# Norms at a batch's end in other places, layer-1 statistics in output frames, and attention sources sent through DRAM

## The chip, the core and the metric

The program runs on one core of one Trainium2 chip. The core has TensorE (matmuls, PE in the profile; its weight loads are PEld), VectorE (DVE), ScalarE (ACT), GpSimd (POOL) and SyncE (SP), which issues most transfers. The metric is the device time of one execution in microseconds (us). The kernel before takes 3635.57 us, the median of three runs (3635.41 to 3636.2). Its profiled execution has a span of 3630.0 us, and TensorE's granted clock was 1.000 of full speed throughout.

## The reference, cut to what matters

Two graph layers on x (8 batches, 2048 nodes, 256 features) with one adjacency matrix (2048 x 2048):

```python
h = relu(layernorm(x))
# layer 0: 4 heads of 64, softmax over each chunk of 256 keys
q, k, v = h @ Wq.T + bq, h @ Wk.T + bk, h @ Wv.T + bv
scores = clip(q k / 8, -10, 10); scores = where(adj == 0, -10, scores)
ctx = sum over 8 chunks of softmax(scores of the chunk) @ v
x = x + layernorm(ctx @ Wo.T + bo + h) * gamma + beta
# layer 1: one head, additive scores
h = relu(layernorm(x)) @ W
e = leaky_relu(e_src[:, None] + e_dst[None, :], 0.01), -1e9 where adj == 0
x = x + relu(softmax(e) @ h)
```

Here e_src and e_dst are h times the two halves of a vector a. In layer 1 a weight exp(leaky_relu(s + d)) is built, up to a factor that cancels, as the larger of two products: a source row times a number of the target, against another number of the target. So the kernel needs, for each block of 512 nodes, the source values exp(0.99 s) as one row of 512 that is repeated on all 128 partitions.

## The kernel before

**Blocks and batches.** A batch's 2048 nodes are four blocks of 512 (`NB`), each four tiles of 128 (`TB`). The blocks are named zero, low, mid and last. For each batch the kernel runs the attention of layer 0, then a stretch that is called the batch's end here, then the products of layer 1. While a batch is in layer 0 or in its end, the projections of the next one (`ahead`) are made.

**Attention.** It has 32 steps (4 blocks x 8 chunks). A frame f, made of `begin(f)` and `end(f)`, holds logits of step f-1, clips (VectorE, L449), exps (ScalarE, L458), sums of pairs of exps (GpSimd, L464), values matmuls of steps f-2 and f-3 (L425), the reciprocal of the sum (L469, L470), the scaling (VectorE, L479) and, from a block's second chunk on, a transfer that adds the scaled product `prod` to `ctxT` (GpSimd's queue, L484). There is one buffer for `prod`.

**Places.** Other work is put into the frames by a hand-written list: `at(n, piece)` puts a piece at place n, where place 2f is the first half of frame f and 2f+1 its second half. A block takes 16 places (`PER`), attention 64 (`STEPS2`). The kind of a piece says where in the half frame it runs: `first` ahead of everything, `pe` beside the matmuls, `mid` between two clips, and without a kind late in the frame's second half (in front of two exps for an even place, behind the logits for an odd one).

**Beside the frames.** `Between` is one block's work after its attention: `residual` (ScalarE relus of the normed input, L291), `bias`, `output_tiled` (projection by Wo, L633), `take_tiles`, `stats`, `power`, `shift`, `scaled` (layer norm), `gamma`, `beta`, `add`. Then come the statistics for layer 1: `stats1` (VectorE, two instructions for each tile, L268 and L269), `power1` (ScalarE), `shift1` (GpSimd within frames) and `norm1` (ScalarE relus). `beside` lists these for blocks zero, low and mid at places counted from the next block's start. The output projection lies at places 8 and 9, so in each later block there is one output frame, in which TensorE has about 3.8 us more to do. The last block's pieces stand in the program's main loop, from place 64 on, and behind the frames.

**Layer 1.** `values` and `keep` make the rows `g` and the two numbers of each node, `sd[:, 0]` (source) and `sd[:, 1]` (target). These have nodes on partitions. `sources(nb)` turns the source column of a block into a row on all partitions: four transposes on TensorE of a column that is repeated 128 times (L815) into one bank of PSUM, and an exp on ScalarE (L819) into a tile `src` of the tag `hn`, which has five buffers. `weights` (VectorE, L825 and L831) makes four tiles of weights from `src`, and `products` (TensorE, L848) multiplies them with `g`. Each block has four such pieces, 16 for a batch, with weights made two pieces ahead. `finish` scales the sums, adds the mean for nodes without neighbours and adds to x on GpSimd (L865). Blocks 0 and 1 have their `sources` at the batch's end in seven batches (`ahead` exists), blocks 2 and 3 in the loop, at the second piece of the block before. In the last batch that of block 1 stands before the first products.

**Queues.** Each engine runs its instructions in the order of the program. SP's queue issues loads of x and of the mask `bound`, stores of the output, and empty instructions (`fence`, L381) that order matmuls which write one bank.

Of the kernel before, what the change touches and what calls it, by code (L numbers as in the profile page):

```python
# [8 lines left out]
F32 = mybir.dt.float32  # L9
# [8 lines left out]
P = 128  # L18
# [10 lines left out]
def gnn_two_layers(  # L29
# [38 lines left out]
    def ps_s():  # L68
        return ps.tile([P, 2, 512], F32, tag="s", name="ps_s")
# [10 lines left out]
    def ps_m():  # L80
        if turn_about[0]:
            turn_about[1] += 1
            if turn_about[1] % 2:
                return ps_n()
        return ps_t()
# [28 lines left out]
    kept = ctx.enter_context(tc.tile_pool(name="kept", bufs=1, space=bass.MemoryType.DRAM))  # L114
    bound_d = [kept.tile([P, NT, NB], I8, name=f"bound_d{nb}") for nb in range(NNB)]
    bounds, bounds1 = {}, {}

    def bound_tile():
        return xpool.tile([P, NT, NB], I8, tag="bound", name="bound", bufs=2)
# [472 lines left out]
    class Between:  # L592
# [151 lines left out]
        def beside(self):  # L744

            todo = {
                -3: [self.load],
                3: [lambda: self.residual(0)],
                4: [lambda: self.residual(1)],
                5: [lambda: self.bias(0)],  # L750
                6: [lambda: self.bias(1)],
                8: [pe(lambda: self.output_tiled(0)), lambda: self.stats([0]), lambda: self.beta(0)],
                9: [
                    pe1(lambda: self.output_tiled(1)), mid_clips(lambda: self.take_tiles(0)),
                    mid_clips(lambda: self.take_tiles(1)), lambda: self.stats([1]),
                ],
                10: [lambda: self.stats([2]), lambda: self.beta(1)],
                11: [lambda: self.stats([3])],
                12: [self.power],
                13: [self.shift],  # L760
                14: [lambda: self.scaled(range(TB))],
                15: [lambda: self.gamma(0)],
                16: [lambda: self.gamma(1)],
                18: [lambda: self.add(0)],
                20: [lambda: self.add(1)],
            }

            def at(n, *pieces):
                todo.setdefault(n, []).extend(pieces)

            if self.nb == NNB - 2:
                return todo
            for t, n in enumerate((20, 22, 26, 28)):
                at(n, lambda t=t: self.stats1([t]))
            at(29, self.power1)
            at(30, self.shift1)
            if self.nb == 1:
                at(31, lambda: self.norm1(0))
                at(32, lambda: self.norm1(1))
            return todo  # L780


    class Layer1:
# [21 lines left out]
        def targets(self, t0=0, t1=NT):  # L805
            d = self.sd[:, 1, t0:t1]
            nc.scalar.activation(self.cd[:, 0, t0:t1], d, AF.Exp)
            nc.scalar.activation(self.cd[:, 1, t0:t1], d, AF.Exp, scale=SLOPE, bias=negshift)

        def sources(self, nb):  # L810

            pt = ps_m() if nb < 2 or nb % 2 else ps_s()[:, 0, :]
            for i in range(TB):
                t = TB * nb + i
                nc.tensor.transpose(  # L815
                    pt[:, i * P:(i + 1) * P], self.sd[:, 0, t:t + 1].to_broadcast([P, P]), ident
                )
            self.src[nb] = work.tile([P, NB], F32, tag="hn", name="src", bufs=5)
            nc.scalar.activation(self.src[nb], pt, AF.Exp, scale=1.0 - SLOPE, bias=negshift)  # L819
# [33 lines left out]
        def finish(self, nb, accs, store=False):  # L853
            x4 = self.blocks[nb].x4
            for t in range(TB):
                acc = accs[t]
                rz = small.tile([P, 1], F32, tag="rz1", name="rz1")
                nc.vector.tensor_scalar(rz, acc[:, F:F + 1], 1e-37, None, op0=ALU.max)  # L858
                nc.vector.reciprocal(rz, rz)
                r = work.tile([P, F], F32, tag="r", name="r")  # L860
                nc.scalar.activation(r, acc[:, 0:F], AF.Relu, scale=rz)
                nc.vector.scalar_tensor_tensor(
                    r, self.average, lone[:, nb * TB + t:nb * TB + t + 1], r, op0=ALU.mult, op1=ALU.add
                )
                nc.gpsimd.tensor_tensor(x4[:, t, :], x4[:, t, :], r, op=ALU.add)  # L865
                if store:
                    at = (nb * TB + t) * P
                    nc.sync.dma_start(out[self.b, at:at + P, :], x4[:, t, :])
# [122 lines left out]
    for b in range(B):  # L991
# [40 lines left out]
        at(3 * PER + 4, lambda: fetch(bounds1, 0))  # L1032
        at(STEPS2 + 2, lambda: fetch(bounds1, 1))
        at(STEPS2 - 6, last.load)
        at(STEPS2 - 1, lambda: last.residual(0))

        late = 0 if ahead else 3
        at(STEPS2 + late, lambda: last.residual(1))
        at(STEPS2 + 1, lambda: last.bias(0))
        at(STEPS2 + 2 + late, lambda: last.bias(1))  # L1040
        at(STEPS2 + 3, lambda: last.beta(0))
        at(STEPS2 + 4, lambda: last.beta(1))
        at(STEPS2 + 2, pe(lambda: low.turn1(0)), pe(lambda: low.turn1(1)))
        at(STEPS2 + 3, first(lambda: low.keep1(0)), first(lambda: low.keep1(1)))
        if ahead:
# [32 lines left out]
        if ahead:  # L1078
            for t in range(TB):
                mid.stats1([t])  # L1080
                low.values(t)
                low.keep(t)
            mid.power1()
            mid.shift1()
            ahead.load(2)
            ahead.turn(1, 0)
            ahead.turn(1, 1)
            mid.norm1(0)
            mid.norm1(1)
            ahead.norm(2, 0)  # L1090
            ahead.values(0)
            last.output(0)
            last.output(1)
            last.take(0)
            last.take(1)
            ahead.norm(2, 1)
            ahead.load(3)
            mid.ends(0)
            last.stats(range(TB))
            ahead.qk(1, 0)  # L1100
            last.power()
            last.shift()
            last.scaled(range(TB))
            ahead.qk(1, 1)
            for t2 in range(2):
                last.gamma(t2)
                last.add(t2)
            for t in range(TB):
                last.stats1([t])
                mid.values(t)  # L1110
                mid.keep(t)
            last.power1()
            last.shift1()
            ahead.turn(2, 0)
            ahead.turn(2, 1)
            last.norm1(0)
            last.norm1(1)
            ahead.values(1)
            zero.norm1(0)
            zero.norm1(1)  # L1120
            ahead.norm(3, 0)
            ahead.qk(2, 0)
            zero.ends(0)
            ahead.norm(3, 1)
            ahead.qk(2, 1)
            zero.ends(1)
            ahead.turn(3, 0)
            ahead.turn(3, 1)
            ahead.values(2)
            last.ends(0)  # L1130
            ahead.qk(3, 0)
            last.ends(1)
            one.total()
            one.targets()
            one.sources(0)
            one.sources(1)
            ahead.qk(3, 1)
            weights(0)
            one.mean()
            weights(1)  # L1140
            ahead.values(3)
        else:
            for t in range(TB):
                zero.values(t)
                zero.keep(t)
                mid.stats1([t])
            one.targets(0, TB)
            one.sources(0)
            mid.power1()
            mid.shift1()  # L1150
            low.ends(1)
            weights(0)
            mid.norm1(0)
            mid.norm1(1)
            one.targets(TB, 2 * TB)
            last.output(0)
            last.output(1)
            weights(1)
            last.take(0)
            last.take(1)  # L1160
            mid.ends(0)
            mid.ends(1)
            last.stats(range(TB))
            last.power()
            last.shift()
            last.scaled(range(TB))
            one.targets(2 * TB, 3 * TB)
            one.sources(1)
            accs[0] = one.accumulators(0)
            early(0)  # L1170
            for t2 in range(2):
                last.gamma(t2)
                last.add(t2)
            last.stats1(range(TB))
            last.power1()
            last.shift1()
            weights(2)
            last.norm1(0)
            last.norm1(1)
            early(1)  # L1180
            last.ends(0)
            last.ends(1)
            early(2)
            one.total()
            one.targets(3 * TB, NT)
            weights(3)
            one.mean()
            weights(4)

        far = projs[b + 2] = Projection(b + 2) if b + 2 < B else None  # L1190
        for i, (nb, j4) in enumerate(pieces1):
# [3 lines left out]
                weights(i + 2)  # L1195
            if nb not in accs:
                accs[nb] = one.accumulators(nb)
            if j4 == 1 and nb + 1 < NNB and nb + 1 not in one.src:
                one.sources(nb + 1)
            one.products(accs[nb], ws.pop(i), j4)  # L1200
            if j4 == 0 and nb > 0:
                one.finish(nb - 1, accs[nb - 1])
# [53 lines left out]
```

The softmax here doesn't subtract the row's maximum and nothing guards it: scores larger than these inputs give would overflow.

## Time and profile before

| from the profile of the kernel before | us |
|---|---|
| span | 3630.0 |
| TensorE busy | 3594.1 |
| VectorE busy | 2577.4 |
| ScalarE busy | 1961.8 |
| GpSimd busy | 1791.5 |
| attention of the second batch, 983 to 1229 us: TensorE busy | 246.00 of 246.00 |
| products of the second batch, 872.46 to 963.5 us: TensorE busy | 91.04 of 91.04 |
| last batch's end, 3475 to 3530 us: TensorE busy | 48.42 of 55.00 |
| first 90 us: TensorE busy | 70.88 of 90.00 |

The rows for stretches come from a table by stage of the trace. A row of a group of instructions reads: line, engine, operation, output and inputs by their names, shapes, count, then the busy time in us and the mean length of one in ns, and then idle time of the engine just before them with what ended it. A listed length of a matmul spans its way through the pipeline, and matmuls overlap: what one takes of TensorE's stream is the distance from its start to the next one's start. A row of the timeline reads: start in us, length in us, engine, line, operation, tiles, count, and in brackets the idle time before it.

### The profile page before, as it was taken

The page shows a single profiled execution, that of the slowest core. Times are in us where ns is not written, and L with a number is a line of the kernel's source. Part 1 is how long each engine was busy: PE and PEld are TensorE (multiplying, and loading weights), DVE is VectorE, ACT ScalarE, POOL GpSimd, SP SyncE. Part 2 cuts the span into 40 slices and gives each one's busy share as a digit, 9 for nine tenths or more (in the row PEclk, how much of TensorE's full clock was granted, in tenths as well). Part 3 has the DMA queues.
Part 4 walks back from the last instruction along what each step waited for, and adds up shares of the span by engine and source line. Part 5 has one row for each costly group of instructions (what it writes and reads, how often), then busy time and mean ns, then how long its engine had stood idle before and what let it go on. Part 6 is the DMA issues. An engine that isn't in the chain of part 4 may idle for free.

```text
span 3630.0 us, 104929 instructions
## 1 busy us (share of the span) xinstructions
PE 3594.1 (99%) x46640; PEld 2205.1 (61%) x46640; DVE 2577.4 (71%) x3963; ACT 1961.8 (54%) x2975; POOL 1791.5 (49%) x1142
## 2 busy tenths in 40 slices
PE   7999999999999999999999999999999999999999
PEld 4444785547745577555874458645586555864568
DVE  5887577866778666786667866678576785757866
ACT  5677416774167732677236762377713767146650
POOL 0678016870178702786037850378403784047731
PEclk9999999999999999999999999999999999999999
DMA  7444113340134411343113431134312442124321
GB/s 226 116 103 101 41 53 84 83 108 28 64 84 87 98 37 57 84 101 83 47 48 83 101 77 47 53 84 95 79 51 59 89 90 59 47 54 89 76 55 35
DMA packets 133302, 277.27 MB, mean 76 GB/s; under 512 B 26608, under 2 KB 91888, under 8 KB 124656
## 3 DMA queue, kind: packets, MB, share of 16 engines
q0 software_dynamic: 32256, 117.45, 17.7%
q1 hardware_dynamic: 83952, 151.01, 12.2%
q8 instruction: 365, 5.98, 0.7%
q10 hardware_dynamic: 16640, 2.10, 0.4%
q14 instruction: 89, 0.73, 0.1%
HBM read 132.12 MB, written 20.97 MB: 42 GB/s over the span
## 4 chain that ended last, share of the span: by engine, by line
PE 97%; DMA 1%; ACT 1%; DVE 1%; issue 0%; POOL 0%; ACTq 0%; POOLq 0%; SPq 0%; DVEq 0%
PE ps_s L409 24%; PE ps_n L425 24%; PE ps_s L848 12%; PE ps_t L437 6%; PE ps_n L848 6%; PE ps_t L848 6%; PE ps_t L633 2%; PE ps_t L353 2%; PE ps_n L353 2%; PE ps_s L353 2%; PE ps_t L721 2%; PE ps_n L721 2%; PE ps_t L367 1%; PE ps_n L367 1%; PE ps_t L300 1%; PE ps_n L300 1%
## 5 line engine op out<-in xcount | busy, mean ns | idle before, releaser
L464 POOL TENSOR_TENSOR both<-e 128x1024 f32<-128x1024 f32 x512 | 1219.8, 2411 | 646.9 <-PE ps_t L437 340.1
L449 DVE SCALAR_TENSOR_TENSOR e<-ps_s,bound 128x1024 f32<-128x1024 f32 x1024 | 1223.7, 1220 | 404.6 <-PE ps_s L409 401.5
L409 PE MATMUL ps_s<-q,k 64*32 64x512 f32 x16384 | 1434.1, 590 | 2.1 <-DVE e L449 2.1
L458 ACT ACTIVATE e<-e 128x1024 f32<-128x1024 f32 x1024 | 1050.5, 1051 | 545.4 <-DVE e L449 529.6
L425 PE MATMUL ps_n<-e,v 64*32 64x512 f32 x16384 | 1220.5, 590 | 4.8 <-ACT e L458 2.3
L425 PEld LDWEIGHTS ps_n<-e,v 64*32 64x32 f32 x16384 | 451.9, 107 | 482.1 <-issue 391.9
L409 PEld LDWEIGHTS ps_s<-q,k 64*32 64x32 f32 x16384 | 451.9, 106 | 468.2 <-issue 325.4
L865 POOL TENSOR_TENSOR x<-x,r 128x256 f32<-128x256 f32 x128 | 98.7, 771 | 1135.9 <-DVE rz L858 1004.8
L437 PE MATMUL ps_t<-both,ones 64*32 64x512 f32 x4096 | 539.0, 591 | 0.6
L848 PE MATMUL ps_s<-g,w 128*128 128x257 f32 x2048 | 448.6, 380 | 0.0
L848 PEld LDWEIGHTS ps_s<-g,w 128*128 128x128 f32 x2048 | 387.7, 190 | 55.5
L479 DVE TENSOR_TENSOR prod<-ps_n,rz 128x512 f32<-128x512 f32 x448 | 288.5, 686 | 169.1 <-PE ps_n L425 85.1
L831 DVE SCALAR_TENSOR_TENSOR w<-bound,w 128x1024 f32<-128x1024 int8 x256 | 313.7, 1225 | 8.7
L848 PE MATMUL ps_n<-g,w 128*128 128x257 f32 x1024 | 292.4, 382 | 0.0
L848 PE MATMUL ps_t<-g,w 128*128 128x257 f32 x1024 | 289.7, 380 | 0.0
L825 DVE TENSOR_SCALAR w<-src,cd 128x512 f32<-128x512 f32 x512 | 265.3, 561 | 9.8 <-ACT src L819 9.4
L469 ACT ACTIVATE rz<-ps_t 128x512 f32<-128x512 f32 x256 | 153.0, 598 | 166.5 <-PE ps_t L437 128.4
L484 POOL DMA_DIRECT2D ctxT<-prod x224 | 194.7, 869 | 52.5 <-DVE prod L479 50.9
L848 PEld LDWEIGHTS ps_n<-g,w 128*128 128x128 f32 x1024 | 192.2, 190 | 43.9 <-issue 17.6
L848 PEld LDWEIGHTS ps_t<-g,w 128*128 128x128 f32 x1024 | 193.8, 189 | 28.1
L437 PEld LDWEIGHTS ps_t<-both,ones 64*32 64x32 f32 x4096 | 115.2, 106 | 92.7 <-SPq L381 47.0
L470 ACT ACTIVATE rz<-rz 128x512 f32<-128x512 f32 x256 | 161.8, 632 | 8.1
(130 smaller groups left out, 2882.3 us busy)
## 6 DMA issues: line engine op xcount, KB each, us to landing
ctxT<-prod POOLq DMA_DIRECT2D x224, 512.0 KB, 4.8
bound<-bound_d SPq DMA_DIRECT2D x62, 1024.0 KB, 5.1
xp<-in_x_dram SPq DMA_DIRECT2D x60, 512.0 KB, 4.6
rows<-in_adj_dram SPq DMA_DIRECT2D x32, 512.0 KB, 5.2
x<-in_x_dram SPq DMA_DIRECT2D x32, 512.0 KB, 4.7
out_dram<-x SPq DMA_DIRECT2D x31, 512.0 KB, 2.9
bound_d<-bound_part ACTq DMA_DIRECT2D x16, 128.0 KB, 4.5
bound_d<-bound SPq DMA_DIRECT2D x2, 1024.0 KB, 6.2
```

The lines of the kernel that those rows point to most:

```text
L353: nc.tensor.matmul(pp, w[:, di, do * P:(do + 1) * P], self.hT[nb][:, di, :], start=di == 0, stop=di == FC - 1,)
L409: nc.tensor.matmul(self.s[n, o][c * Q:(c + 1) * Q, kt, :], self.k[p][rows, at:at + Q], self.q[p][rows, nb * NB:(nb + 1) * NB], start=True, ...
L425: made.append(nc.tensor.matmul(self.num[n, c][h * Q:(h + 1) * Q, :], self.v[rows, j * KT + kt, at:at + Q], self.e[n, p][rows, i * KT + kt, :],
L437: nc.tensor.matmul(self.total[n][h * Q:(h + 1) * Q, :], ones[rows, :], self.both[n, h // 2][rows, h % 2, :], start=half == 1, stop=half == 0,)
L449: nc.vector.scalar_tensor_tensor(self.e[n, p][:, i * KT:(i + 1) * KT, :], self.s.pop((n, o)), -CLIP * SC, bounds[nb][:, j * KT:(j + 1) * K ...
L458: nc.scalar.activation(e, e, AF.Exp, scale=1.0 / SC)
L464: nc.gpsimd.tensor_tensor(self.both[n, p], e[:, 0], e[:, 1], op=ALU.add)
L479: nc.vector.tensor_tensor(dst[:, c, :], self.num.pop((n, c)), self.rz[n], op=ALU.mult)
L484: nc.gpsimd.dma_start(self.ctxT[nb], self.prod.pop(n), accum_op=ALU.add)
L825: nc.vector.tensor_scalar(w[:, i, :], self.src[nb], self.cd[:, 0, j:j + 1], self.cd[:, 1, j:j + 1], op0=ALU.mult, op1=ALU.max,)
L831: nc.vector.scalar_tensor_tensor(two, bounds1[nb][:, j - 1:j + 1, :], 0.0, two, op0=ALU.is_gt, op1=ALU.mult)
L848: nc.tensor.matmul(accs[t][:, 0:F + 1], w[:, i, t * P:(t + 1) * P], g[:, j, :], start=j == 0, stop=j == NT - 1,)
```

## The change

It has four parts.

1. **Sources by transfers.** `sources` stays for block 0 of each batch. For blocks 1, 2 and 3, `send` writes the source column (128 partitions x 4 numbers) to a small tensor in DRAM in the order of the nodes, `receive` loads it as one row of 512 to all partitions, straight into a `src` tile, and `received` takes the exp in place on ScalarE. It is for doing this turn without TensorE and PSUM.
2. **Layer-1 statistics.** `stats1` of blocks zero and low moves from places 20, 22, 26 and 28 to one tile at 22 and three at 25, which is the second half of the next block's output frame, ahead of its clips. `power1` and `shift1` come three places earlier, and so does `norm1` of block low. It is for using frames in which VectorE has less to do than TensorE.
3. **Norms at the batch's end.** The last block's `residual`, `bias` and `beta` come one place later (in the last batch the second `residual` and `bias` stay where they are), so that fewer of ScalarE's norms stand at one place.
4. **The last stores.** In the last batch's last block the addition to x runs on VectorE in place of GpSimd.

```diff
+    source_d = [kept.tile([TB, P], F32, name=f"source_d{nb}") for nb in range(NNB)]
...
-            for t, n in enumerate((20, 22, 26, 28)):
-                at(n, lambda t=t: self.stats1([t]))
-            at(29, self.power1)
-            at(30, self.shift1)
+            at(22, lambda: self.stats1([0]))
+            at(25, first(lambda: self.stats1([1, 2, 3])))
+            at(26, self.power1)
+            at(27, self.shift1)
             if self.nb == 1:
-                at(31, lambda: self.norm1(0))
-                at(32, lambda: self.norm1(1))
+                at(28, lambda: self.norm1(0))
+                at(29, lambda: self.norm1(1))
...
+        def send(self, nb):
+            nc.sync.dma_start(source_d[nb].rearrange("t p -> p t"), self.sd[:, 0, TB * nb:TB * (nb + 1)])
+        def receive(self, nb):
+            self.src[nb] = work.tile([P, NB], F32, tag="hn", name="src", bufs=5)
+            nc.sync.dma_start(
+                self.src[nb], source_d[nb].rearrange("(o t) p -> o (t p)", o=1).to_broadcast([P, NB])
+            )
+        def received(self, nb):
+            src = self.src[nb]
+            nc.scalar.activation(src, src, AF.Exp, scale=1.0 - SLOPE, bias=negshift)
...
-            pt = ps_m() if nb < 2 or nb % 2 else ps_s()[:, 0, :]
+            pt = ps_m()
...
-                nc.gpsimd.tensor_tensor(x4[:, t, :], x4[:, t, :], r, op=ALU.add)
+                adder = nc.vector if store else nc.gpsimd
+                adder.tensor_tensor(x4[:, t, :], x4[:, t, :], r, op=ALU.add)
...
-        at(STEPS2 - 1, lambda: last.residual(0))
-        late = 0 if ahead else 3
-        at(STEPS2 + late, lambda: last.residual(1))
-        at(STEPS2 + 1, lambda: last.bias(0))
-        at(STEPS2 + 2 + late, lambda: last.bias(1))
-        at(STEPS2 + 3, lambda: last.beta(0))
-        at(STEPS2 + 4, lambda: last.beta(1))
+        at(STEPS2, lambda: last.residual(0))
+        late = 0 if ahead else 2
+        at(STEPS2 + 1 + late, lambda: last.residual(1))
+        at(STEPS2 + 2, lambda: last.bias(0))
+        at(STEPS2 + 3 + late, lambda: last.bias(1))
+        at(STEPS2 + 4, lambda: last.beta(0))
+        at(STEPS2 + 5, lambda: last.beta(1))
...
             zero.ends(1)
+            one.send(1)
+            one.send(2)
...
             last.ends(0)
+            one.receive(1)
             ahead.qk(3, 0)
             last.ends(1)
...
             one.sources(0)
-            one.sources(1)
             ahead.qk(3, 1)
             weights(0)
             one.mean()
             weights(1)
+            one.send(3)
+            one.receive(2)
             ahead.values(3)
...
-            one.sources(1)
+            one.send(1)
+            one.receive(1)
             accs[0] = one.accumulators(0)
...
             one.mean()
+            one.received(1)
+            one.send(2)
+            one.send(3)
+            one.receive(2)
...
-            if j4 == 1 and nb + 1 < NNB and nb + 1 not in one.src:
-                one.sources(nb + 1)
+            if j4 == 1 and nb + 1 < NNB:
+                one.received(nb + 1)
+            if j4 == 2 and nb == 1:
+                one.receive(3)
```

## The prediction

> **What bounds the kernel now.** First the page: busy shares, the line of TensorE in the 40 slices, and the chain.
>
> ```profile
> PE 3594.1 (99%) x46640; PEld 2205.1 (61%) x46640; DVE 2577.4 (71%) x3963; ACT 1961.8 (54%) x2975; POOL 1791.5 (49%) x1142
> ...
> PE   7999999999999999999999999999999999999999
> ...
> PE 97%; DMA 1%; ACT 1%; DVE 1%; issue 0%; POOL 0%; ACTq 0%; POOLq 0%; SPq 0%; DVEq 0%
> ```
>
> TensorE is busy or owns the chain nearly everywhere, and the one weak slice is the start, which the change leaves alone. So the questions are: which TensorE instructions leave, and which of its waits change?
>
> Second, TensorE's own groups and the timeline around the instructions that leave (start, length in us):
>
> ```profile
> L815 PE MATMUL ps_n<-ident,sd 128*128 128x128 f32 x64 | 9.6, 272 | 0.0
> L815 PE MATMUL ps_t<-ident,sd 128*128 128x128 f32 x32 | 5.0, 274 | 0.3 <-DVE sd L730 0.3
> L815 PE MATMUL ps_s<-ident,sd 128*128 128x128 f32 x32 | 4.8, 273 | 0.0
> ```
>
> ```profile
> 461.58 0.60 PE L848 MATMUL ps_t<-g,w 128*128 128x257 f32 x2
> 462.01 0.60 PE L815 MATMUL ps_s<-ident,sd 128*128 128x128 f32 x4
> 462.45 0.60 PE L848 MATMUL ps_n<-g,w 128*128 128x257 f32 x2
> ```
>
> A group of four transposes starts at 462.01 and its successor at 462.45: it takes 0.44 us of the stream, though each is listed at 272 to 274 ns. The groups at 418.67, 419.11 and 490.22 have the same distance; finer starts give 0.435 us. Nothing waits before or after them, so they are pure cost.
>
> Third, the waits (waiter, releaser: us in total, times, longest):
>
> ```profile
> DVE prod L479 <- DMA ctxT<-prod: 55.8, 58, 7.2
> ...
> DVE stats L268 <- POOL x L691: 9.0, 7, 1.3
> ```
>
> The first is the only wait that spreads into TensorE within attention: a late accumulate of ctxT holds `prod`, then ps_n, then the next values matmuls. The second is at each batch's end, beside other TensorE work.
>
> Fourth, one output frame on VectorE:
>
> ```profile
> 758.56 1.23 DVE L449 SCALAR_TENSOR_TENSOR e<-ps_s,bound 128x1024 f32<-128x1024 f32 x1 [2.10 <-PE ps_s L409]
> ```
>
> VectorE stands idle for 2.10 us before the second clip of that frame, because TensorE is doing the output projection.
>
> **What the Trainium skill says.** (1) Perfetto Trace Analysis, Identifying the Most-Contended Engine: matmul busy time is a poor measure of distance to roofline, since matmuls are pipelined. The trace agrees (a listed 273 ns against a spacing of 109 ns), so I price by starts. (2) TensorE: Matmul & The Clock Gate, Part 2, Step-by-step: back to back, a matmul costs about one cycle for each column. The spacings agree: 128 columns 109 ns, 257 columns 217 ns. (3) The same page, Part 4: a PE transpose measured about 275 ns, mostly access latency; the listed 273 ns agree, and are not the price here. (4) DMA: Bandwidth & Descriptors, Specifications: transfers under 512 B are read-modify-write. The new send writes 4-byte elements; no run here shows that.
>
> **The change, part by part.**
>
> *Transposes.* 128 run; only block 0 of each batch keeps its four. 8 batches x 3 blocks = 24 groups x 0.435 us = **10.4 us** off TensorE. In the seven batches with a successor, all three groups stand in an unbroken stream (PE idle before L815 is 0.3 us over all). In the last batch they start at 3506.45, 3547.9 and 3575.79, also with products right behind. I count all 24.
>
> *Send and receive in their place.* 48 transfers on SP's queue. What waits on them: the exp in `received` on ScalarE, then the weights on VectorE. Nearest rows: a 1 KB column load lands in 3.9 to 4.3 us, a row broadcast to 128 partitions in 4.4 to 5.6 us. Taking the larger twice, 11.2 us from send to data; the lower end, an out_dram store of 128 KB (1.7) plus 4.2, is 5.9. Block 1's receive can be issued from about 411 us in the first batch (transposes of `last.ends(0)` at 410.88), so its data are there by 422. ScalarE reaches that exp after `mean` (424.04) and is then idle for 16.9 us; VectorE reads the block-1 source first at 442.24. Slack 18 us. Blocks 2 and 3 are asked for more than 10 us ahead (block 3 one block step of 20 us, three pieces of 6.95 us). Even at four times my lower end nothing waits. Taken: 0.
>
> Behind these transfers on SP: the x loads of the batch after next, which run as early as 402 us now and will be issued at about 420. Their reader, a statistic on VectorE, is at 439.10; a load lands in 4.6 us. The fences of attention also pass through SP's queue, but none stands between a send and its receive. 0.
>
> The exp itself: 0.67 to 0.68 us from PSUM before, the same size from SBUF after. 0.
>
> *Layer-1 statistics.* Four pairs (0.42 + 0.18 us, one each 0.53 us) go from places 20, 22, 26, 28 of a block to 22 and 25 (a place is half a frame). The three at place 25 need about 1.7 us and fit into the hole of 2.10 us shown above; behind them wait the clip, and for the clip the logits, so they cost nothing as long as they stay under it. The relieved places had extra statistics and VectorE waits on `prod`. Summing, over all half frames of 3.86 us, what the eight batches have above the best of them, I get about 13 us of scattered stalls, mostly 0.2 to 1 us where a ctxT accumulate landed late. GpSimd's order, which causes most of them, hardly changes. I take 0.5 us off, bounds +4 and -6.
>
> *Norms at the batch's end.* Two relus (1.08 us) of ScalarE leave place 63 for 64, and four of block 1 leave 63 and 64 for 60 and 61. In seven batches TensorE shows no wait there beyond transitions between tiled and full matmuls (0.4 to 0.7 us each), which stay: 0. In the last batch there is less beside work. The bias on GpSimd (3473.20, 1.24 us to the next start) stands before the pair of adds and the last-but-one ctxT transfer (3479.09). Moved behind it, the second add still needs an exp that ends at 3476.02, so the transfer leaves at about 3478.4: 0.7 us earlier, and TensorE waits for exactly this (1.43 us before the transposes at 3485.41). **0.7 us**, bounds 0 and 1.4. The extra relus at 60 and 61 could cost the last batch up to 1 us, because its block 0 norms stand at 58 and 59; I leave that in the range.
>
> *Last add on VectorE.* After the last matmul the chain is max, reciprocal, relu, multiply-add, add, store, and the store of 128 KB lands in 1.7 us. GpSimd's add takes 0.72 us from 3626.58; VectorE's 128x256 adds take 0.42 us (L648) and need no hop. **0.4 us**, bounds 0.2 and 0.6.
>
> Sum: 10.4 + 0.5 + 0.7 + 0.4 = 12.0; 3635.6 - 12.0 = **3623.6 us**.
>
> **The rivals.**
>
> A: the scattered stalls shrink too. For it: VectorE's waits on the transfer are 58, and fewer statistics per place let it catch up. Against: the transfer's landing, not VectorE, ends those waits. Half of 13 us more: about 3617.
>
> B: TensorE is freed, but the time comes back as waits: ScalarE's crowded places 60 and 61 (in one frame of 7.7 us the four exps of 1.05 and the reciprocal's 0.60 and 0.63, 5.4 us, plus four relus and one `power`, 2.9 us) delay exps by about 1 us in each of 8 batches. Against: places 62 and 63 now hold more (scaled, two pairs of relus, a copy) and show no TensorE wait. 3623.6 + 8 = about 3631.5.
>
> C: slower. A send of 512 four-byte writes takes some 30 us instead of 5, or holds SP's queue; then ScalarE waits in `received`, the weights stop, and the products with them: at 2 us per batch 3640, at 4 us 3656. Against: the slack of 18 us, and that column loads with the same four-byte elements land in 4.3 us. Taken at 3642.
>
> **From these to the numbers.** Forecast 0.75, A 0.10, B 0.08, C 0.07. The forecast's own width is its bounds: -6 to +4 from stalls, about 1 from the last batch. The range 3618 to 3629.5 takes in nearly all of it and a part of A. Faster by over 0.2% means under 3628.3: the forecast and A, 0.85. Within 0.2%: B, 0.08. Slower: C, 0.07.
>
> **What would show it.** L815 with 32 transposes; the loop of layer 1 from the first product to the last shorter by 0.87 us in each batch, and the batch's end by 0.44; ScalarE's wait for the source transfer near zero in all but odd cases; PE's idle sum unchanged within 2 us; no TensorE wait on VectorE in output frames. It is wrong if weights wait for the source transfers, if a clip of place 25 holds the logits, or if stalls on ctxT change by more than 5 us.

## The result, and the profile after

| | us |
|---|---|
| before, median of six runs | 3635.49 (3630.91 to 3636.81) |
| after, median of six runs | 3622.85 (3619.28 to 3624.78) |
| after / before | 0.9966, 95% interval 0.9953 to 0.9978 |
| difference | -12.6, forecast -12.0 |
| span of the profiled executions | 3630.0 before, 3622.7 after |

The forecast held. But the single profiled execution gained only 7.3 us, and the way to its sum is not quite the one that was forecast. Line numbers below are those of the kernel whose profile is shown: a line of before stands some lines further down in the changed kernel. The page of the changed kernel, read in the same order as before: busy shares, TensorE in 40 slices, the chain, and from the table of issues (tiles, queue, operation, count, KB each, us to landing) the transfers of the sources.

```profile
PE 3587.4 (99%) x46544; PEld 2202.7 (61%) x46544; DVE 2580.6 (71%) x3967; ACT 1960.9 (54%) x2975; POOL 1788.1 (49%) x1138
...
PE   8999999999999999999999999999999999999999
...
PE 96%; DMA 2%; ACT 1%; DVE 1%; issue 0%; POOL 0%; ACTq 0%; SPq 0%; DVEq 0%; POOLq 0%
...
src<-source_d SPq DMA_DIRECT2D x24, 256.0 KB, 4.8
```

TensorE runs 96 matmuls fewer and still bounds the kernel; DMA's part of the chain went from 1% to 2%. A receive lands in 4.8 us (median; 3.0 to 10.7). From the trace's own table of issues the send, and from the groups of TensorE and ScalarE the transposes and the two kinds of exp:

```profile
source_d<-sd SPq DMA_DIRECT2D x24, 2.0 KB, 8.9
```

```profile
L832 PE MATMUL ps_t<-ident,sd 128*128 128x128 f32 x32 | 5.0, 274 | 0.3 <-DVE sd L732 0.3
...
L825 ACT ACTIVATE src<-src,negshift 128x512 f32<-128x512 f32 x24 | 17.1, 712 | 0.0
...
L836 ACT ACTIVATE src<-ps_t,negshift 128x512 f32<-128x512 f32 x8 | 5.4, 670 | 0.0
```

A send of 2 KB takes 8.9 us (median; 7.9 to 11.1), longer than any other transfer of that table, the largest of which have 1024 KB. Its packets are over 1.2 to 2.4 us after the issue; what is late is the signal that they have landed. Still ScalarE never stood idle ahead of L825 (the last column is 0.0): the slack was enough. So far the plan worked. The waits of the changed kernel (waiter, releaser: us in total, times, longest) show what did not:

```profile
DVE prod L481 <- DMA ctxT<-prod: 38.8, 50, 1.6
...
DVE stats L270 <- POOL x L693: 9.0, 7, 1.3
...
DVE w L842 <- ACT src L825: 3.4, 1, 3.4
...
PE ps_n L723 <- DVE o L658: 3.1, 1, 3.1
PE ps_t L613 <- DMA ctxT<-prod: 3.0, 1, 3.0
```

The last line is new. L613 is the output projection of a last block, and it happened in one batch of eight, the fourth. (`PE ps_n L723 <- DVE o L658: 3.1`, in the last batch, was there before too. `DVE w L842 <- ACT src L825: 3.4` is in the last batch as well and is no wait for a transfer: that source had landed at 3500.6, but its exp stands behind `mean`, whose matmuls start at 3526.47. TensorE did not wait there.)

**By stage.** I measured from the start of a batch's last half frame with logits to the next batch's first; this is the batch's end with its layer 1, and it holds all the 24 removed groups of transposes but the last batch's three.

| stretch | before | after |
|---|---|---|
| up to the first logits | 69.3 | 71.8 |
| attention, eight batches | 2198.9 | 2197.8 |
| batch's end and layer 1, each of six batches | 171.38 | 169.71 |
| the same, fourth batch | 171.38 | 174.51 |
| last batch, to the start of the last matmuls | 156.67 | 155.02 |
| after that | 5.40 | 5.29 |

The first row is not the change's: over the profiled executions of all kernels it lies between 69.3 and 72.3, without order. Six batches gained 1.67 us each. The fourth lost 3.13, that is 4.8 us against its neighbours. Here is its timeline, GpSimd's queue and SP's queue first, then TensorE:

```profile
1703.77 0.87 POOL L486 DMA_DIRECT2D ctxT<-prod  x1 [7.53 <-DVE prod L481]
```

```profile
1707.28 0.37 SPq L815 DMA_DIRECT2D source_d<-sd  x1
```

```profile
1713.46 3.50 PE L613 MATMUL ps_t<-woT,ctxT 128*128 128x256 f32 x8 [3.03 <-DMA ctxT<-prod]
1716.80 1.89 PE L613 MATMUL ps_n<-woT,ctxT 128*128 128x256 f32 x8
```

The last accumulate of ctxT leaves at 1703.77. The DMA records say the rest: its semaphore counts 16 times, as many as the page gives the core DMA engines; 15 counts are in by 1708.31, and the last data packet ends by 1708.6, but the 16th count comes at 1713.33. In between, at 1707.28, SP issued the first send, whose 512 four-byte packets moved from 1708.1 to 1708.8. TensorE waits 3.03 us, and then it is slow: the eight matmuls from 1713.46 take 3.34 us to the next group's start, where the same group takes 1.73 in a batch without the wait. The windows (stretch, us, busy us and count of PE, PEld, DVE, ACT, POOL, then PE clock, DMA share, GB/s) show the clock in the column before the last two. First one of before, in the same stretch of its fourth batch's end, then two of the changed kernel:

```profile
1710.00:1715.00 5.00, 5.00 (x25) 4.36 (x24) 2.02 (x4) 3.53 (x8) 0.00 (x0) 1.00 0.00 0
```

```profile
1710.00:1715.00 5.00, 1.97 (x7) 1.33 (x6) 0.69 (x1) 1.57 (x4) 0.00 (x0) 0.82 0.04 3
1715.00:1720.00 5.00, 5.00 (x24) 4.12 (x23) 1.93 (x5) 1.92 (x5) 0.00 (x0) 0.84 0.00 0
```

So 3.0 us of wait cost 3.0 + 1.6 us. The Trainium skill, TensorE: Matmul & The Clock Gate, Part 1, What's actually happening, says that an idle window of about 3.4 us halves TensorE's clock until a busy window has passed. The trace agrees in kind: 3.03 us of wait were enough here, and the matmuls behind it took 3.34 / 1.73 = 1.9 times as long. The length does not agree: in a later run of the same kernel (e3) 2.4 us were enough (0.82 and 0.84 again), while 2.0 us in e1 left the clock at 1.00.

**Why the fourth batch.** In five of the seven batches the last packet of that ctxT transfer ends 4.2 us after its issue, and the first packet of the send starts at 4.37 to 4.40: they miss each other by 0.2 us. In the fourth batch the last packet ends at 4.8, among the packets of the send. It is late there in 11 of the 13 profiled executions (4.5 to 4.8 us, with and without sends), each time with a packet of an instruction load that starts 1.4 to 2.0 us after the issue; in the two without such a packet (e7 and e8 below) it ends at 4.2. To overlap the send is not enough by itself: in the fifth batch the last packet was later still (5.5) and its count came 0.3 us behind it, as usual. That difference stays open.

**The same on one queue.** The receive of block 2 leaves 0.5 us behind the send of block 3. In all eight batches its data packets are over 2.8 to 4.7 us after its issue, but it counts as landed only at 8.5 to 10.7, 0.2 to 0.8 us behind the send; the other 16 receives land at 3.0 to 6.2. This cost nothing, because that source is not yet needed.

### The profile page after: what moved, and what is told of

Read it like the earlier page. It is cut to its first block, busy times and chain, and to the rows that moved or that the text cites. A ratio compares the mean times of both kernels' runs of the same rounds, so it can differ in the third digit from the quotient of the medians.

```text
span 3622.7 us, 104823 instructions
## 1 busy us (share of the span) xinstructions
PE 3587.4 (99%) x46544; PEld 2202.7 (61%) x46544; DVE 2580.6 (71%) x3967; ACT 1960.9 (54%) x2975; POOL 1788.1 (49%) x1138
## 4 chain that ended last, share of the span: by engine, by line
PE 96%; DMA 2%; ACT 1%; DVE 1%; issue 0%; POOL 0%; ACTq 0%; SPq 0%; DVEq 0%; POOLq 0%
PE ps_s L411 24%; PE ps_n L427 24%; PE ps_s L865 12%; PE ps_t L439 6%; PE ps_n L865 6%; PE ps_t L865 6%; PE ps_t L635 2%; PE ps_t L355 2%; PE ps_n L355 2%; PE ps_s L355 2%; PE ps_t L723 2%; PE ps_n L723 1%; PE ps_t L369 1%; PE ps_n L369 1%; PE ps_t L302 1%; DMA ctxT<-prod 1%
## 5 line engine op out<-in xcount | busy, mean ns | idle before, releaser
L842 DVE TENSOR_SCALAR w<-src,cd 128x512 f32<-128x512 f32 x512 | 265.2, 560 | 10.7 <-ACT src L836 6.9
L275 ACT ACTIVATE krn<-mv,eps 128x4 f32<-128x4 f32 x32 | 9.5, 296 | 292.7 <-DVE mv L271 292.7
L439 PEld LDWEIGHTS ps_t<-both,ones 64*32 64x32 f32 x4096 | 115.2, 106 | 85.8 <-SPq L383 42.4
```

The lines of the kernel that those rows point to most:

```text
L439: nc.tensor.matmul(self.total[n][h * Q:(h + 1) * Q, :], ones[rows, :], self.both[n, h // 2][rows, h % 2, :], start=half == 1, stop=half == 0,)
L842: nc.vector.tensor_scalar(w[:, i, :], self.src[nb], self.cd[:, 0, j:j + 1], self.cd[:, 1, j:j + 1], op0=ALU.mult, op1=ALU.max,)
```

## The experiments

The theory was: the transposes give what was forecast; the send's small packets hold back the count of the ctxT transfer in the fourth batch; and the remaining gain of 0.35 us in a batch comes from the norms, not from the transposes. The main rivals were that the fourth batch's loss is chance, or that it is due to the norms' and statistics' new places. A ratio is to the kernel before on the same chip.

**One part of the change at a time.** The first kernel has part 1 alone, the second parts 2, 3 and 4 without it.

```diff
 e1: as after, but
-            at(22, lambda: self.stats1([0]))
-            at(25, first(lambda: self.stats1([1, 2, 3])))
+            for t, n in enumerate((20, 22, 26, 28)):
+                at(n, lambda t=t: self.stats1([t]))
...
-        at(STEPS2, lambda: last.residual(0))
+        at(STEPS2 - 1, lambda: last.residual(0))
...
 e2: as after, but
-            one.send(1)
-            one.send(2)
...
+            one.sources(1)
```

> The kernel before with the source transfers alone (statistics, norms and last add as before). Theory 1, each group of four transposes costs its distance between starts: 24 x 0.435 = 10.4 us less than before, about 3625 us, TensorE's stretch from the last logits of a batch to the next batch's first shorter by 1.30 us; in some executions one stall of up to 5 us more behind the last ctxT transfer of a batch. Rival, the gain comes from the statistics and norms: within 2 us of before. Rival, the transfers cost what they save: within 2 us of before, with waits for the source tiles on ScalarE or VectorE.

> The other three parts without the transfers; all sources by transposes. Theory 1: 1 to 4 us less than before, of which about 0.35 us per batch are seen between the last logits and the next batch's first, and 0.4 us in the last add. Rival, the statistics and norms carry the result: 10 us or more less. Rival, they cost time: slower than before.

Transfers only: 3627.83, ratio 0.9977 (0.9968 to 0.9986), -8.4 us where 10.4 were expected. In five batches the stretch is 170.05 or 170.06 (170.22 in the seventh), so 171.38 - 170.06 = 1.32 us for three groups of transposes, against a forecast of 3 x 0.435 = 1.30. The fourth batch again stands out, with 172.28: its 16th count took 8.5 us from the issue and TensorE waited 2.0.

The rest only: 3632.49, ratio 0.9989 (0.9982 to 0.9995), -4.0 us; all seven stretches are 171.02 to 171.04, the count of the fourth batch took 5.1 us and nothing waited. So the late count comes with the transfers, not with parts 2 to 4, and the 0.35 us comes with the latter. They add up: 171.38 - 1.32 - 0.35 = 169.71, which is what the whole change has.

In the last batch, from the transposes behind the first 64 products to the last products, every kernel with transposes takes 103.85 or 103.86 us and every one with transfers (except e9 and e10, which change this stretch) 102.97 or 102.98, 0.88 for two groups. As a whole it is no help: up to its last matmuls e1 takes 157.7 and e2 158.4 us, both longer than before's 156.67, and in both the clock from 3500 to 3530 us is 0.89 (1.00 before), behind that batch's wait of 3.1 us.

**The changed kernel again, and the sends in the other order.** `send(1)` can leave early, because the values of block low (`low.keep1`) are ready long before those of block mid. Behind `send(2)` it must wait for those.

```diff
             zero.ends(1)
-            one.send(1)
             one.send(2)
+            one.send(1)
             ahead.turn(3, 0)
```

> The changed kernel itself, for its spread on this chip: two groups, near 3620 and near 3624.5 us, the upper where one wait of TensorE for the last ctxT transfer of a batch (3 us, then 1.6 us at a lower clock) occurred. If there are no two groups, the wait is not what spreads the times.

> The changed kernel with the sends of blocks 2 and 1 swapped in seven batches, so that SP holds the first send until block 2's numbers exist, some 19 us later, when the last ctxT transfer has landed. Theory 2, the four-byte writes of the send hold back the last of the 16 counts of that ctxT transfer: no stall of TensorE before the output projection of the last block, executions near 3620 us, none near 3624.5; median 2 to 4 us under the changed kernel. Rival, the late transfer is chance and has nothing to do with the send: the same spread and median as the changed kernel. Rival, the later send makes the source late: block 1's exp waits, slower.

The changed kernel: 3625.23, ratio 0.9972 (0.9962 to 0.9983); the fourth stretch 173.98, 16th count after 8.9 us, wait 2.4 us. Swapped: 3622.16, ratio 0.9960 (0.9948 to 0.9973); in the profiled execution both sends leave at 1728.96, all seven stretches are within 169.70 and 169.72, the count takes 5.0 us, and L613 has no wait:

```profile
1706.51 0.87 POOL L486 DMA_DIRECT2D ctxT<-prod  x1 [7.55 <-DVE prod L481]
```

```profile
1728.96 0.92 SPq L815 DMA_DIRECT2D source_d<-sd  x2
```

```profile
1713.01 1.89 PE L613 MATMUL ps_t<-woT,ctxT 128*128 128x256 f32 x8
1714.74 1.89 PE L613 MATMUL ps_n<-woT,ctxT 128*128 128x256 f32 x8
```

The trace is clear about the wait. The medians differ by 3.1 us as they should, but these two intervals overlap, so by time alone it isn't shown here. Two expectations failed: the changed kernel's seven runs (3622.0 to 3630.5) do not fall into two groups, and two of the five swapped runs lie above 3624.5. One of these, 3626.22, is the profiled execution that has no late count: its attention took 2205.3 us, 7.5 more than that of the changed kernel's first profile. So the scattered stalls of attention spread the times at least as much as the late count does.

**Which of the other parts gives 0.35 us.**

```diff
 e5: before, with part 2 alone
+            at(25, first(lambda: self.stats1([1, 2, 3])))
...
 e6: before, with part 3 alone
+        at(STEPS2, lambda: last.residual(0))
...
```

> The kernel before with only the layer-1 statistics moved (and power1, shift1 and block low's norm1 three places earlier). Theory 1: TensorE's output frames keep their 5.93 us, since three pairs fit into the hole of 2.10 us; the stretch from a batch's last logits to the next batch's first loses at most 0.35 us of 171.38; scattered stalls of attention stay between 0 and 4.5 us per batch; total 0 to 3 us under before. Rival: the clip behind the three pairs comes late, output frames longer than 5.93 us, slower. Rival: fewer scattered stalls, 5 us or more under before.

> The kernel before with only the residual, bias and beta of the last block moved. Theory 1: the stretch between attention of two batches shorter by 0 to 0.35 us in seven batches, last batch's end shorter by about 0.7 us (the wait of 1.4 us before the second turn of block zero); total 0.5 to 3 us under before. Rival: no change at all, the relus and the bias were hidden in every batch.

Statistics only: 3631.42, ratio 0.9987 (0.9978 to 0.9995). Norms only: 3631.03, ratio 0.9989 (0.9982 to 0.9995). By medians that is 3.8 and 4.1 us less than before, where 0 to 3 and 0.5 to 3 were expected; e6's last batch, expected shorter, took 157.3 us in its profile (156.67 before), at a clock of 0.94 from 3500 to 3530 us. Each alone has stretches of 171.02 or 171.03, and together (e2) 171.02 to 171.04: either one removes the same 0.35 us, 2.4 in seven batches. The rest of these differences is not explained. It can be followed at the end of the second batch. ScalarE's timeline there, first before, then after:

```profile
793.89 1.08 ACT L291 ACTIVATE hn<-x,rn 128x256 f32<-128x256 f32 x2
794.87 1.09 ACT L291 ACTIVATE hn<-x,krn 128x256 f32<-128x256 f32 x2
795.86 1.99 ACT L458 ACTIVATE e<-e 128x1024 f32<-128x1024 f32 x2
```

```profile
793.27 1.08 ACT L293 ACTIVATE hn<-x,krn 128x256 f32<-128x256 f32 x2
794.81 2.19 ACT L460 ACTIVATE e<-e 128x1024 f32<-128x1024 f32 x2 [0.46 <-DVE e L451]
```

and TensorE's values groups beside them:

```profile
789.57 2.00 PE L425 MATMUL ps_n<-e,v 64*32 64x512 f32 x32
...
796.88 0.63 PE L425 MATMUL ps_n<-e,v 64*32 64x512 f32 x4
```

```profile
789.87 2.00 PE L427 MATMUL ps_n<-e,v 64*32 64x512 f32 x32
...
796.76 0.63 PE L427 MATMUL ps_n<-e,v 64*32 64x512 f32 x4
```

Before, four relus stand ahead of the two exps, and the values group at 796.88 starts when the first exp is done (795.86 + 1.05 = 796.91; 1.05 us is the mean of an exp on the page). After, two relus are left, the exp waits for its clip instead and is done at 795.86, nearly a microsecond ahead of the group. From group to group it is 7.31 us before and 6.89 after, and to the transposes that follow (799.47 and 799.42) 9.90 and 9.55: the 0.35 us. Before, both `norm1` of block low (part 2) and `residual` of block last (part 3) brought relus to this spot, which fits that taking either away is enough.

**The send's packets by themselves.** The kernel before, with 24 additional transfers that nobody reads, each some 2 us behind the issue of one ctxT transfer and 6 us ahead of the next; 2 KB in 4-byte pieces in one kernel, 64 KB in rows of 512 B in the other.

```diff
+    def probe(i):
+        nc.sync.dma_start(probe_d[i].rearrange("t p -> p t"), ident[:, 0:4])   # 4 bytes
+        nc.sync.dma_start(probe_d[i], ident)                                   # or 512 bytes
...
+            if f in (8, 16, 24):
+                probe(f // 8 - 1)
```

> The kernel before with an added transfer in frames 8, 16 and 24 of each batch (24 in all), about 1.5 us behind the issue of a ctxT transfer: 128 partitions x 4 numbers of the identity to DRAM in elements of 4 bytes, as a send writes them, read by nobody. Theory 2, writes of 4 bytes to DRAM hold back counts of a transfer on the same DMA engines: these 24 ctxT transfers count out at 8 us or later instead of about 4.5, TensorE waits 2 to 4 us behind each, 50 to 120 us slower. Rival, the added transfer only shares bandwidth (0.5 us of packets): under 10 us slower.

> The same at the same places, but the transfer writes the whole identity in rows of 512 bytes (64 KB, 128 packets). Theory 2 with small writes as the cause: ctxT transfers at most 1 us later, under 20 us slower though 32 times the bytes. Rival, any write to DRAM in front of the counts holds them back as long: as slow as the probe with 4 bytes.

With 4-byte pieces: 3767.73, ratio 1.0361 (1.0341 to 1.0382). That is 132 us, 5.5 for each transfer of 2 KB. With rows of 512 B: 3637.76, ratio 1.0007 (0.9998 to 1.0016), although 32 times as many bytes are moved. Landing of the ctxT transfers, and VectorE's waits for them, with 4-byte pieces:

```profile
DMA to landing us min/median/max: 4.5/4.8/16.8
```

```profile
DVE prod L488 <- DMA ctxT<-prod: 123.9, 62, 11.5
```

and the landing with rows of 512 B:

```profile
DMA to landing us min/median/max: 4.5/4.8/6.7
```

The median is the same in both and in before (4.8); only the transfers next to a probe are late. In 18 of 24 cases the packets of the next ctxT transfer themselves ran late and ended 6.3 to 16.6 us after its issue (6.1 at most before). In four, one of them among the 18, the transfer issued ahead of the probe had its packets over by 4.7 us and its last count at 7.0 to 12.4, as in the fourth batch. In three neither is seen. So a probe delays another queue's transfer in two ways, and the one that the sends showed is the rarer. (Not all of the 132 us is shown to come through these transfers: TensorE's listed waits for `prod` before values matmuls are 42.4 us, and 13 waits of 21.9 us together have no releaser in the trace.)

The probe is written on SP's queue, the accumulate on GpSimd's: two queues, and the first delays the second. For the count alone, the Trainium skill, DMA: Bandwidth & Descriptors, Queues, rings and completion order, names a mechanism: the semaphore increment of a transfer is a strongly ordered write, which lands only after every earlier write of that DMA engine, across its queues. This case agrees with it: in the fourth batch all data were over at 1708.6 and the count came 4.7 us later. For the late packets of the 18 cases no cause is shown. The two probes differ in the number of packets too (512 against 128). The number by itself does not make a store slow: the output's stores of 512 packets of 1 KB land in 2.9 us. But pieces between 4 and 512 B were not tried. A probe costs more than the change's own sends do on average, since it meets a transfer nearly every time and a send does so in one batch of eight.

**A better version.** Two things are left to take: the send's order, and the 3.1 us of the last batch (`PE ps_n L723 <- DVE o L658`), where VectorE makes layer-1 weights ahead of two instructions that TensorE waits for.

```diff
 e9: last batch
-            weights(1)
             last.take(0)
             last.take(1)
+            weights(1)
 e10: this, and the sends swapped as in e4
 e11: the changed kernel, a third time
```

> The changed kernel with one more edit in the last batch: `last.take` (VectorE) ahead of the second piece of weights. In the changed kernel TensorE waits 3.1 us there for the take, which stands behind 4.3 us of weights. Theory: that wait falls under 0.7 us and the tail after the last logits (155.0 us) to about 152.5; where a wait of 3 us was followed by a lower clock, up to 3 us more; median 2 to 5 us under the changed kernel. Rival: the weights become late in its place, the first products wait, no gain.

> The changed kernel with the sends of blocks 2 and 1 swapped in seven batches and with `last.take` ahead of the second piece of weights in the last. Theory: both gains add, tail near 152.5 us, all seven stretches between attentions at 169.71 us; about 3618 us, a ratio to before of 0.995 or less, 4 to 8 us under the changed kernel on the same chip. Rival: the swap only moves the waits, no better than the early take alone.

> The changed kernel again, on the chip of the two others, to compare with them: between 3619 and 3630 us, ratio to before near 0.997; one stretch between attentions of 173 us or more in most executions, at the fourth batch.

On one chip: e9 3624.59, ratio 0.9971 (0.9961 to 0.9980); e10 3617.16, 0.9953 (0.9941 to 0.9966); e11 3627.67, 0.9978 (0.9969 to 0.9986). The last batch's tail went from 155.0 to 150.6 in e9 and e10, more than the wait of 3.1 (152.5 was expected); the wait is gone, and from 3475 to 3530 us the clock is 1.00 in e10 where the changed kernel had 0.97.

The late count came again in e11 (10.3 us, stretch 175.36, wait 3.7). In the profiled run of e9 it came at 6.2, late but soon enough that TensorE did not wait. So all five profiles with the early send have it (6.2 to 10.3, in e1, in e9 and in three of the changed kernel), and those of e4 and e10, with the late send, do not (5.0 and 5.1).

Between e10 and e11 are 10.5 us, more than the 4 to 8 expected; in the profiled executions the two places give 5.65 (175.36 against 169.71) and 4.5. e9 and e10 differ in the order of the sends alone, and here the time shows it too: 3624.59 against 3617.16, and only two of e9's ten runs are below the slowest of e10's five. The early take alone (e9 against e11) has 3.1 us between the medians, but overlapping intervals. The fourth batch's end in e11 and in e10:

```profile
1690.00:1745.00 55.00, 51.24 (x264) 31.17 (x253) 17.79 (x51) 33.52 (x75) 13.29 (x10) 0.97 0.26 64
```

```profile
1690.00:1745.00 55.00, 54.97 (x282) 35.65 (x281) 19.31 (x57) 34.84 (x79) 11.74 (x10) 1.00 0.24 61
```

TensorE is busy for 51.24 of 55 us in the one and 54.97 in the other, with 18 matmuls more in the record. e10 is faster than both kernels: its interval lies below that of e11, and its ratio to before is 0.9953 where the changed kernel had 0.9966, 0.9972 and 0.9978.

## Why the prediction was right, step by step

| step | forecast | measured |
|---|---|---|
| transposes, seven batches | 9.1 | 9.2 = 7 x 1.32 |
| send and receive | 0 | -4.8, in the fourth batch |
| statistics, scattered stalls | 0.5 | 1.1, but see below |
| norms, seven batches | 0 | 2.4 = 7 x 0.35, shared with the statistics |
| last batch: transposes 1.3, norms 0.7 | 2.0 | 1.65 = 1.3 + 2.0 - 1.7 at a lower clock |
| last add | 0.4 | 0.1 |
| sum | 12.0 | 9.7 |

Leaving out the start-up, the profiled pair differs by 7.3 + 2.5 = 9.8 us, which the sum accounts for. The medians differ by 12.6, and the interval of the ratio means 8.0 to 17.1 us. Both the forecast and the sum lie within it. The two later sets of runs of the same kernel lie 11.3 us (e3) and 7.3 us (e11) under the medians of before on their chips. That the forecast is so near the first median is partly luck: its errors have opposite signs, gains of 2.4 and 1.3 us in the norms and losses of up to 4.8 us to the send and 1.7 to the clock, none of which it saw.

*Transposes: right*, and in the way they were priced. Start to start 0.435 us for a group gave 1.30 for three; the listed 273 ns for each matmul would have given 3.3. Its own sign came true too: from the first product to the last, layer 1 went from 117.96 to 117.08 us in each of seven batches, 0.88 where 0.87 was forecast. Its second citation agrees with the spacings only in proportion (217 / 109 = 2.0 = 257 / 128); that a column takes one cycle is not shown by them.

*Last batch: right in its sum only.* The two groups of transposes that can be measured apart gave 0.88 us. The wait before the transposes of block zero fell from 1.43 to 0.75 us, 0.7 as forecast:

```profile
PE ps_n L302 <- DVE prod L481: 0.8, 1, 0.8
```

But from the last half frame to these transposes the batch gained 2.0 us in all (17.8 before, 15.8 after); an earlier wait for `prod` of 0.54 is gone as well, and the rest was not followed up. The clock took 1.7 back: behind the wait of 3.14 us for L723, which both kernels have, the 64 products took 13.88 us before and 15.07 after, and the matmuls ahead of them lost another 0.5. The same wait stands in 11 of the 13 profiled executions; two of them lost nothing behind it (before, e7), six 1.7 us, three (e1, e2, e4) 2.8 to 3.0. Why it differs is not shown.

*Send and receive: the step that failed*, "the fences of attention also pass through SP's queue, but none stands between a send and its receive. 0." The slack of the sources was right: send 8.9 and receive 4.8 us, 13.7 together, against a slack of 18, and ScalarE had no wait. The landing estimate (5.9 to 11.2 for both) was low by 2.5 us against these medians. What it did not ask is who else shares the DMA engines: it followed SP's queue and the readers of the data, not a transfer of another queue, whose count the send held to 9.6 us. Rival C had the slow 4-byte writes, but put the wait at the sources' reader, where it never was.

*Statistics: right in their cost, wrong in the cause given.* The hole in the output frame held three pairs. After the change VectorE's timeline reads

```profile
756.69 0.42 DVE L270 BATCH_NORM_STATS2 stats<-x 128x6 f32<-128x256 f32 x1
757.14 0.18 DVE L271 BATCH_NORM_AGGREGATE mv<-stats 128x2 f32<-128x6 f32 x1
...
758.20 0.18 DVE L271 BATCH_NORM_AGGREGATE mv<-stats 128x2 f32<-128x6 f32 x1
758.87 1.22 DVE L451 SCALAR_TENSOR_TENSOR e<-ps_s,bound 128x1024 f32<-128x1024 f32 x1 [0.49 <-PE ps_s L411]
```

The three pairs end at 758.38, and the clip behind them still waits 0.49 us for TensorE, not the other way round. The half frames of the output frames keep their lengths (5.59 and 5.93 us). But the scattered stalls were put down to GpSimd's order. The traces point elsewhere: every ctxT transfer whose last packet was later than 5.3 us has a packet of an instruction load running while its own do (31 of 31 before, 28 of 28 after; of all 224 transfers before, some 130 have one). That is seen together and wasn't tried, since the change doesn't control when these loads come. The stalls move from batch to batch, and attention as a whole takes between 2197.8 and 2205.3 us in the profiled executions of all kernels but the one with 4-byte probes; the difference of 1.1 us between one run of before and one of after is nothing within that.

*Norms and statistics: the seven batches gave 0.35 us each, where the prediction took 0.* It read no TensorE wait there beyond transitions, and took these as fixed. The wait was for an exp behind four relus, and too small to be listed as one.

*Last add: mis-sized.* The add took 0.42 in place of 0.72 us as forecast, but the previous tile's add now stands on the engine of the chain:

```profile
3617.74 0.42 DVE L883 TENSOR_TENSOR x<-x,r 128x256 f32<-128x256 f32 x1
3618.08 0.15 DVE L875 TENSOR_SCALAR rz<-ps_t 128x1 f32<-128x1 f32 x1
```

The last tile's first instruction (L875) starts as that add ends, 0.68 us after the start of the last matmul group; before it was 0.42. So 0.26 of the 0.4 went back.

*Rivals.* B (time given back at places 60 and 61) didn't appear: the stretches of the batch's end became shorter. A (stalls shrink by half) didn't either. One of the signs of being wrong did, in part: VectorE's waits for ctxT fell from 55.8 to 38.8 us, more than 5. Seven waits of 2.3 to 3.0 us at the batches' ends and one of 7.2 in the last are gone, and others grew; TensorE's attention became shorter by 1.1 us only, so most of this had cost TensorE nothing.

## What to carry to other kernels

Pricing the removed matmuls by the distance between starts, in a stage where TensorE has no waits, was exact to 0.02 us in a batch. When a transfer is added, ask not only who waits for its data but which other transfers are under way while it runs: 4-byte pieces held them up here and rows of 512 B did not, so write small results in such rows if that is possible, and if not, issue them when no awaited transfer is under way. A wait of 2.4 us or more in a busy TensorE often cost 1.6 to 3.0 us beyond itself here, so such waits are among the first to remove.

## What the runs showed of the hardware

- A store to DRAM of 2 KB in 512 pieces of 4 B landed 8.9 us after its issue (7.9 to 11.1), one of 64 KB in rows of 512 B in 3.6 (2.6 to 4.8).
- That store held back the count of transfers whose packets were already over: of another queue's in the fourth batch (9.6 us instead of about 4.5), and of the load issued 0.5 us behind it on its own queue in eight of eight batches (8.5 to 10.7 us, data over by 4.7 at the latest). The packets' own records don't show it; only the difference between the last data packet and the 16th count does.
- With probes of the same kind, mostly the packets of the next transfer were late themselves: in the one that counted out at 16.8 us, the last packet ended at 16.6. Per probe this cost 5.5 us.
- In the fourth batch the last packet of this transfer is a little late (4.5 to 4.8 us instead of 4.2) in 11 of 13 executions, all with a packet of an instruction load beside it, and not in the two without. So it meets the send there; in the fifth batch a meeting of the same kind held nothing, and why stays open.
- Behind waits of 3.0 and 2.4 us the granted clock was 0.82 and 0.84 over two windows of 5 us; behind one of 2.0 us it was 1.00. Behind the same wait of 3.14 or 3.15 us in 11 executions the lower clock cost 0, 1.7, or 2.8 to 3.0 us.
